# Turning the normed residual with VectorE blocks and a trip through DRAM instead of TensorE transposes

## The chip, the cores and the metric

The kernel runs on one core of one Trainium2 chip. Five engines work side by side, each through its own queue in order: TensorE (PE; its weight loads are listed as PEld), VectorE (DVE), ScalarE (ACT), GpSimd (POOL) and SyncE (SP). In this kernel nearly all DMAs are issued by SP, and an issue that waits for a semaphore holds up every issue behind it. The metric is the device time of the core in microseconds, the median of several executions.

## The reference

One transformer block in fp32 over 2048 tokens of 1024 features, with a single attention head of 256 features:

```python
x = x + layernorm(attn(layernorm(x)))
x = x + layernorm(ffn(layernorm(x)))

# attn: qkv = x @ Wqkv + bqkv; softmax(q k^T / 16) @ v; @ Wo + bo      (d = 256)
# ffn:  (silu(x @ W_gate.T) * (x @ W_up.T)) @ W_down.T                 (F = 2752)
# layernorm: (x - mean) / sqrt(var + 1e-5), no weights
```

The second layernorm's input is what this case is about. Its result, one row per token, has to be turned so that features lie on the partitions, because the gate and up matmuls sum over features.

## The kernel before

**Number format.** Each fp32 product is done as three fp32r matmuls (high times high, high times low, low times high). So operands are split into a high part (ScalarE copy, L110) and a low part (VectorE subtraction, L111) by `split`. The gate, up and down products are further cut by a Strassen scheme over halves of tokens, features and hidden units (`Pair`, `prod`, `sum_x`, `down_weights`).

**Tiles.** There are 16 tiles of 128 tokens (`NT`), in groups of four (`TB`), and 8 feature blocks of 128 (`NC_`).

**Attention stage (about 143 to 418 us).** The loop at L1201 runs over the 16 tiles in a software pipeline. Iteration i turns the softmax rows of tile i on TensorE (`turn`, L451; split by L110 and L111), computes the scores of tile i+1 (`scores`, L127 to L129, with a maximum on VectorE, L264), its softmax (`softmax`, L439 to L444, exponentials on ScalarE, L442), multiplies by v (`attend`, L467 and L468, into bank 6, read out by L469 and L470), turns the result (`turn_o`, L477, bank 5, read out by L479 and L480) and projects tile i-1 (`proj`, banks 5 and 7, read out by L490). For the first eight tiles (`EARLY`), iteration i also does the residual of tile i-2: `residual` normalizes the attention output in place (L504, ScalarE), adds x (L505, VectorE), stores the row as `x1_d` (L506, SP), takes its statistics (L117, L120 and L121 on VectorE; L122 and L508 on GpSimd) and writes the normed row over the attention output (L509, ScalarE). Then `xpose(i - 2)` turns that row.

**`xpose` before.** For each half of the features, four TensorE transposes (L599) go into one PSUM bank, a ScalarE copy (L601) brings it to the x tile, and one DMA (L603) stores it into `xT_d`, the turned matrix in DRAM. In the attention stage it borrows banks 6 and 5, in the gate-and-up stage banks 4 and 5, which are otherwise idle then.

**After the eight early tiles,** `first_load` (L613) and `first_sums` (L637, L661, L671) read `xT_d` of the first two groups back and build the Strassen operands in the last iterations of the attention loop.

**Gate-and-up stage of the first 1024 tokens (about 418 to 765 us).** The loop at L1312 runs over ten pairs of hidden blocks. Each pair issues 14 products of 12 matmuls (L866). Between products two background jobs run: `ahead(p)` turns the late tile of the pair before, loads the next late tile's attention output (`at_d`, L1294) and x (L1295) and forms weight sums (`down_weights`, L1010 and L880, stored by L1015); `behind(p)` loads weights (L1005) and does `residual` of the late tile (with L505 on GpSimd). So pairs 1 to 8 each do the residual of one of tiles 8 to 15, and the pair after each turns it. Weights stream through a ring of raw tiles (`raws`: `f4[4]`, `f2p`, `wr`; L769) into slots. Results are stored by `put` (L897).

**Order.** The tile framework's scheduler sets each engine's order from its own estimate of times, except where an instruction is pinned in program order (`pin`); the source order of the loops is therefore a guide and not the order of the queues.

**Buffers.** `pair[t % 3]` holds tile t's two rows: `a` (attention output, then normed row) and `xt` (x, then the residual). Late tiles use `f4[2]` and `f4[3]`.

Of the kernel before, what the change touches and what calls it, by code (L numbers as in the profile page):

```python
# [8 lines left out]
F32 = mybir.dt.float32  # L9
# [6 lines left out]
P = 128  # L16
T = 2048
C = 1024
D = 256
F = 2752  # L20
NT = T // P
# [3 lines left out]
TB = G // P  # L25
# [9 lines left out]
def block_kernel(ctx, tc, x, xt, wqk, wqk_t, wv, bqk, bv, wo, bo, wgu, wlast, wd, out):  # L35
# [12 lines left out]
    nc = tc.nc  # L48
# [4 lines left out]
    def tl(p, shape, dt, name):  # L53
        return p.tile(shape, dt, tag=name, name=name, bufs=1)
# [3 lines left out]
    ident = tl(cpool, [P, P], F32, "ident")  # L58
# [18 lines left out]
    bank = [tl(bank_pool, [P, 512], F32, f"bank{i}") for i in range(8)]  # L77

    dram = ctx.enter_context(tc.tile_pool(name="dram", bufs=1, space=bass.MemoryType.DRAM))
    q_d = [tl(dram, [P, 2, G], F32, f"q_d{g}") for g in range(NG)]  # L80
    mr_d = [tl(dram, [P, 2 * TB], F32, f"mr_d{g}") for g in range(NG)]
    xT_d = [tl(dram, [C, G], F32, f"xT_d{g}") for g in range(NG)]
    at_d = [tl(dram, [P, C], F32, f"at_d{t}") for t in range(NT)]
    x1_d = [tl(dram, [P, C], F32, f"x1_d{t}") for t in range(NT)]
    hd = [[{n: tl(dram, [P, 512], F32, f"hd{s}_{p}_{n}") for n in HS} for p in range(NPAIR)] for s in range(2)]
    xs_d = [[tl(dram, [P, C], F32, f"xs_d{c}_{k}") for k in range(2)] for c in range(NC_ // 2)]
    td = [{n: tl(dram, [P, 512], F32, f"td{p}_{n}") for n in ("T1", "T2", "T3", "T4")} for p in range(NPAIR)]
# [7 lines left out]
    f4 = [tl(cpool, [P, C], F32, f"f4_{i}") for i in range(5)]  # L95
# [17 lines left out]
    def norm_stats(halves, pin=None):  # L113

        s = small_tile()
        for i, h in enumerate(halves):
            b = nc.vector.bn_stats(s[:, 6 * i : 6 * i + 6], h)  # L117
            if pin:
                pin(b)
        nc.vector.bn_aggr(s[:, 12:14], s[:, 0:12])  # L120
        nc.vector.tensor_scalar(s[:, 14:15], s[:, 13:14], EPS, None, ALU.add)  # L121
        nc.gpsimd.tensor_tensor(s[:, 15:16], s[:, 14:15], mhalf, ALU.pow)  # L122
        return s[:, 12:13], s[:, 15:16], s
# [133 lines left out]
    def scores(i, j, pin=lambda i: i):  # L257

        cols = slice((i % TB) * P, (i % TB + 1) * P)
        q = qa if i < TB else qs[(i // TB) % 2]  # L260
        for d in range(2):
            k = kT(d, j)
            mm3(bank[j], (q[:, d, 0, cols], q[:, d, 1, cols]), (k[:, 0, :], k[:, 1, :]), d == 0, d == 1, pin)
        nc.vector.tensor_reduce(ys[i % 4][:, j : j + 1], bank[j], AX.X, ALU.max)  # L264
# [153 lines left out]
    pair = [(f4[0], f4[1]), (f4[2], f4[3]), (f2p[0], f2p[1])]  # L418
# [3 lines left out]
    EARLY = 2 * TB  # L422
# [5 lines left out]
    def q_load(g):  # L428
        nc.sync.dma_start(qraw, q_d[g])
# [6 lines left out]
    def softmax(i):  # L436

        s = ys[i % 4]
        nc.vector.tensor_reduce(s[:, 4:5], s[:, 0:4], AX.X, ALU.max)  # L439
        nc.vector.tensor_scalar(s[:, 5:6], s[:, 4:5], -1.0 / 16.0, None, ALU.mult)  # L440
        for j in range(4):
            nc.scalar.activation(p_s[:, j * 512 : j * 512 + 512], bank[j], AF.Exp, bias=s[:, 5:6], scale=1.0 / 16.0, accum_out=s[:, 8 + j : 9 + j])  # L442
        nc.vector.tensor_reduce(s[:, 12:13], s[:, 8:12], AX.X, ALU.add)
        nc.vector.reciprocal(s[:, 13:14], s[:, 12:13])  # L444

    def turn(i, j):

        b = bank[(4, 7)[j % 2]]
        for n in range(4):
            k = 4 * j + n  # L450
            nc.tensor.transpose(b[:, n * P : (n + 1) * P], p_s[:, k * P : (k + 1) * P], ident)  # L451
        d = pT[i % 2][:, 4 * j : 4 * j + 4, :, :]
        split(d[:, :, 0, :], d[:, :, 1, :], b.rearrange("p (n q) -> p n q", n=4))
# [41 lines left out]
    def out_stats(t, a):  # L495

        m, r, s = norm_stats([a[:, 0:512], a[:, 512:1024]], tc.keep_in_program_order if t >= EARLY else None)
        nc.gpsimd.tensor_scalar(s[:, 16:17], m, r, -1.0, ALU.mult, ALU.mult)
        return r, s

    def residual(t, a, xt, st=None, pin=lambda i: i):

        r, s = st or out_stats(t, a)
        pin(nc.scalar.activation(a, a, AF.Identity, bias=s[:, 16:17], scale=r))  # L504
        (nc.gpsimd if t >= EARLY else nc.vector).tensor_tensor(xt, xt, a, ALU.add)  # L505
        nc.sync.dma_start(x1_d[t], xt)  # L506
        m, r, s = norm_stats([xt[:, 0:512], xt[:, 512:1024]])
        nc.gpsimd.tensor_scalar(s[:, 16:17], m, r, -1.0, ALU.mult, ALU.mult)  # L508
        nc.scalar.activation(a, xt, AF.Identity, bias=s[:, 16:17], scale=r)  # L509
# [81 lines left out]
        pin(nc.vector.tensor_tensor(wo_s[:, d, 1, :], wr[d], f32(wo_s[:, d, 0, :]), ALU.subtract))  # L591


    def xpose(t, a, b, banks):
        for hf in range(2):
            o = banks[hf]
            for j in range(4):
                cb = 4 * hf + j
                nc.tensor.transpose(o[:, j * P : (j + 1) * P], a[:, cb * P : (cb + 1) * P], ident)  # L599
            s = b[:, hf * 512 : hf * 512 + 512]  # L600
            nc.scalar.copy(s, o)  # L601
            d = xT_d[t // TB][hf * 512 : hf * 512 + 512, (t % TB) * P : (t % TB + 1) * P]
            nc.sync.dma_start(d.rearrange("(j p) t -> p j t", p=P), s.rearrange("p (j t) -> p j t", j=4))  # L603

    def two(t):
        return t.rearrange("p (j n) -> p j n", j=2)
# [56 lines left out]
    def first_load(cb, r1, r2):  # L663
        load_xq(r1, 0, cb)
        load_xq(r2, 1, cb)
# [68 lines left out]
    class Slot:  # L734
        t = None
# [440 lines left out]
    X, Y = bank[0:4], bank[4:8]  # L1176
# [24 lines left out]
    for i in range(NT):  # L1201
        more = i + 1 < NT
        if i % TB == 0 and TB <= i < NT - TB:
            q_load(i // TB + 1)
        turn(i, 0)
        turn(i, 1)
        if i == NT - 1:
            for f in order[:2]:
                f.use()
            for f, r in zip(order[4:6], f4[2:4]):  # L1210
                f.load(r)
        if more:
            scores(i + 1, 0)
            scores(i + 1, 1)
        turn(i, 2)
        turn(i, 3)
        if more:
            scores(i + 1, 2)
            scores(i + 1, 3)
            softmax(i + 1)  # L1220

        if i < 2:
            wo_split(i)
        if i == 1:
            q_load(1)
        if i == 2:
            q_split(1, pin)
        if i % TB == 0 and TB <= i < NT - TB:
            q_split(i // TB + 1, pin)
        if 2 <= i < EARLY + 2:  # L1230
            residual(i - 2, *pair[(i - 2) % 3], sts[i - 2], pin)
        if i < EARLY:
            nc.sync.dma_start(pair[i % 3][1], x[i * P : (i + 1) * P, :])
        if i == NT - 1:
            for f in order[2:5]:
                f.use()
            for f, r in zip(order[6:8], (wr[1], f4[1])):
                f.load(r)
        if i > 0:
            turn_o(i - 1)  # L1240
        attend(i)
        if i > 0:
            proj(i - 1)
        if 2 <= i < EARLY + 2:
            xpose(i - 2, *pair[(i - 2) % 3], (bank[6], bank[5]))
        if 0 < i <= EARLY:
            sts[i - 1] = out_stats(i - 1, pair[(i - 1) % 3][0])
        cb = i - EARLY - 3
        if 0 <= cb < 4:
            first_sums(cb, *room[cb % 2])  # L1250
        if 0 <= cb + 1 < 4:
            first_load(cb + 1, *room[(cb + 1) % 2])
        if i == NT - 4:
            feed.pump()
        if i == NT - 2:
            for n in range(2):
                slots.free(flat(a2[:, 2 * n : 2 * n + 2, :, :]))
            feed.pump()
            order = [t2[0], t13[0], t13[1], t13[2], t2[1], t13[3]] + t4
            spare = f4[2], f4[3], wr[1], xe  # L1260
            for f, r in zip(order, spare):
                f.load(r)
# [17 lines left out]
    def late(p):  # L1280
        return EARLY + p - 1 if 1 <= p <= NT - EARLY else None

    def ahead(p):
        if p == 0:
            with tc.issue_after(last_o[0].ins):
                for n in range(5, 8):
                    order[n].use()
                    if n == 5:
                        order[9].load(f4[3])
            return  # L1290
        if late(p - 1):
            xpose(late(p - 1), *f4[2:4], Y[0:2])
        if late(p):
            nc.sync.dma_start(f4[2], at_d[late(p)])  # L1294
            nc.sync.dma_start(f4[3], x[late(p) * P : (late(p) + 1) * P, :])  # L1295
        down_weights(p - 1)

    def behind(p):
        if p == 0:
            for n in range(8, 10):  # L1300
                order[n].use()
            raws2.free(wr[1])
            raws2.free(bo_s)
        with tc.issue_after(pairs[1][0].loading.ins) if p == 0 else nullcontext():
            load_down(p)
        if late(p):
            residual(late(p), *f4[2:4])

    for s in range(2):
        pairs, rest, dn = half[s]  # L1310
# [70 lines left out]
```

## Time and profile before

| What | Value |
|---|---|
| Median of 3 runs | 1659.46 us (1659.44 to 1659.66) |
| Span of the profiled execution, first to last instruction | 1658.2 us |
| Rest of the time, outside that span (median less span) | 1.3 us |
| TensorE busy | 1647.1 us, 99% |
| VectorE busy | 1104.2 us, 67% |
| ScalarE busy | 734.7 us, 44% |
| GpSimd busy | 108.2 us, 7% |
| Mean granted TensorE clock | 0.999 |
| DMA traffic | 283.62 MB, mean 171 GB/s |

The profile is one execution; its own time is given by its span, and 1.3 us more lie around it. Busy shares are means over stages. A line such as L866 can be that of a helper through which many products go. In the chain of waits a row gives its start, its length and the engine and line. "Idle before" names what ended an engine's wait.

### The profile page before, as it was taken

The page shows a single profiled execution, that of the slowest core. Times are in us where ns is not written, and L with a number is a line of the kernel's source. Part 1 is how long each engine was busy: PE and PEld are TensorE (multiplying, and loading weights), DVE is VectorE, ACT ScalarE, POOL GpSimd, SP SyncE. Part 2 cuts the span into 40 slices and gives each one's busy share as a digit, 9 for nine tenths or more (in the row PEclk, how much of TensorE's full clock was granted, in tenths as well). Part 3 has the DMA queues.
Part 4 walks back from the last instruction along what each step waited for, and adds up shares of the span by engine and source line. Part 5 has one row for each costly group of instructions (what it writes and reads, how often), then busy time and mean ns, then how long its engine had stood idle before and what let it go on. Part 6 is the DMA issues. An engine that isn't in the chain of part 4 may idle for free.

```text
span 1658.2 us, 21110 instructions
## 1 busy us (share of the span) xinstructions
PE 1647.1 (99%) x7704; PEld 1374.3 (83%) x7704; DVE 1104.2 (67%) x1660; ACT 734.7 (44%) x1093; POOL 108.2 (7%) x157
## 2 busy tenths in 40 slices
PE   9999999999999999999999999999999999999998
PEld 8888888888888888888888888888888888888887
DVE  6756677768777777777587458955556665455458
ACT  5663555445544444444365344433333333354342
POOL 3120000000011111111000001100000000000001
PEclk9999999999999999999999999999999999999999
DMA  8451123435656666556477656533222233686653
GB/s 318 167 177 65 62 91 114 151 123 185 235 186 219 216 213 220 196 197 231 141 236 265 192 195 213 193 134 105 95 96 95 96 104 119 228 264 198 196 185 123
DMA packets 137689, 283.62 MB, mean 171 GB/s; under 512 B 14320, under 2 KB 31344, under 8 KB 137584
## 3 DMA queue, kind: packets, MB, share of 16 engines
q1 hardware_dynamic: 136432, 280.30, 50.6%
q10 hardware_dynamic: 1152, 1.97, 0.3%
q8 instruction: 60, 0.98, 0.2%
q14 instruction: 45, 0.37, 0.1%
HBM read 198.31 MB, written 83.90 MB: 170 GB/s over the span
## 4 chain that ended last, share of the span: by engine, by line
PE 96%; DMA 1%; DVE 1%; issue 1%; ACT 0%; SPq 0%; POOL 0%; POOLq 0%; DVEq 0%
PE bank L866 72%; PE bank L127 4%; PE bank L129 4%; PE bank L128 4%; PE bank L467 3%; PE bank L468 2%; PE bank L451 2%; PE bank L245 1%; PE bank L246 1%; PE bank L599 1%; PE bank L310 1%; DMA f<-wv 0%; PE bank L1052 0%; PE bank L1051 0%; PE bank L463 0%
## 5 line engine op out<-in xcount | busy, mean ns | idle before, releaser
L866 PE MATMUL bank<-a 128*128 128x512 f32 (+1 forms) x960 | 226.4, 386 | 0.0
L866 PE MATMUL bank<-xb,a 128*128 128x512 f32 x912 | 212.5, 389 | 0.5 <-DVE a L111 0.5
L866 PEld LDWEIGHTS bank<-a 128*128 128x128 f32 x960 | 179.0, 188 | 36.6
L866 PEld LDWEIGHTS bank<-xb,a 128*128 128x128 f32 x912 | 170.9, 188 | 36.2 <-DVE a L111 0.9
L110 ACT CAST a<-f2p 128x1024 fp32r<-128x1024 f32 (+2 forms) x123 | 107.0, 870 | 113.0 <-PE bank L866 86.3
L111 DVE TENSOR_TENSOR a<-f2p,a 128x1024 fp32r<-128x1024 f32 (+2 forms) x123 | 122.3, 994 | 45.2 <-ACT a L110 40.9
L111 DVE TENSOR_TENSOR a<-f,a 128x1024 fp32r<-128x1024 f32 (+1 forms) x70 | 78.5, 1122 | 103.5 <-ACT a L110 101.3
L866 PE MATMUL bank<-kx,a 128*128 128x512 f32 x612 | 146.0, 389 | 0.0
L866 PEld LDWEIGHTS bank<-kx,a 128*128 128x128 f32 x612 | 114.9, 188 | 23.9
L866 PE MATMUL bank<-wvo 128*128 128x512 f32 (+1 forms) x498 | 120.9, 386 | 0.0
L880 DVE TENSOR_TENSOR p_s<-bank,p_s 128x512 f32<-128x512 f32 x96 | 65.0, 681 | 77.1 <-PE bank L866 47.7
L866 PEld LDWEIGHTS bank<-wvo 128*128 128x128 f32 x498 | 92.9, 188 | 18.9
L110 ACT CAST a<-f 128x1024 fp32r<-128x1024 f32 (+1 forms) x70 | 57.8, 825 | 103.3 <-PE bank L866 101.8
L866 PE MATMUL bank<-kx,wvo 128*128 128x512 f32 x420 | 100.1, 389 | 0.0
L866 PE MATMUL bank<-a,a 128*128 128x512 f32 x420 | 99.4, 389 | 0.0
L866 PEld LDWEIGHTS bank<-kx,wvo 128*128 128x128 f32 x420 | 78.8, 188 | 16.4
L866 PEld LDWEIGHTS bank<-a,a 128*128 128x128 f32 x420 | 78.8, 188 | 16.4
L111 DVE TENSOR_TENSOR wvo<-f,wvo 128x1024 fp32r<-128x1024 f32 (+1 forms) x47 | 54.6, 1162 | 51.0 <-ACT wvo L110 51.0
L866 PE MATMUL bank<-a1b,wvo 128*128 128x512 f32 x360 | 86.6, 389 | 0.0
L866 PEld LDWEIGHTS bank<-a1b,wvo 128*128 128x128 f32 x360 | 67.6, 188 | 14.0
L866 PE MATMUL bank<-kx 128*128 128x512 f32 (+1 forms) x339 | 78.5, 387 | 0.0
L866 PEld LDWEIGHTS bank<-kx 128*128 128x128 f32 x339 | 63.4, 188 | 13.0
(330 smaller groups left out, 3075.5 us busy)
## 6 DMA issues: line engine op xcount, KB each, us to landing
f2p<-wgu SPq DMA_DIRECT2D x41, 512.0 KB, 5.5
hd_S<-p_s SPq DMA_DIRECT2D x60, 256.0 KB, 4.7
f<-x SPq DMA_DIRECT2D x28, 512.0 KB, 4.2
f<-wgu SPq DMA_DIRECT2D x22, 512.0 KB, 3.5
wr<-wgu SPq DMA_DIRECT2D x21, 512.0 KB, 5.8
f<-wd SPq DMA_DIRECT2D x20, 512.0 KB, 5.1
hd_A<-xi SPq DMA_DIRECT2D x40, 256.0 KB, 2.0
td_T<-f SPq DMA_DIRECT2D x40, 256.0 KB, 4.5
```

The source lines that it names most:

```text
L110: nc.scalar.copy(hi, src)
L111: (lo_engine or nc.vector).tensor_tensor(lo, src, f32(hi), ALU.subtract)
L127: pin(nc.tensor.matmul(o, w[0], m[0], start=first, stop=False))
L128: pin(nc.tensor.matmul(o, w[0], m[1], start=False, stop=False))
L129: return pin(nc.tensor.matmul(o, w[1], m[0], start=False, stop=last))
L245: pin(nc.tensor.matmul(b, xg[:, c, 0, cols], wv_s[:, c, :, :].rearrange("p a f -> p (a f)"), start=(c == 0), stop=False))
L246: pin(nc.tensor.matmul(b[:, D:], xg[:, c, 1, cols], wv_s[:, c, 0, :], start=False, stop=(c == 7)))
L451: nc.tensor.transpose(b[:, n * P : (n + 1) * P], p_s[:, k * P : (k + 1) * P], ident)
L467: nc.tensor.matmul(b, p[:, k, 0, :], vt(k).rearrange("p h d -> p (h d)"), start=(k == 0), stop=False)
L468: nc.tensor.matmul(b[:, D:], p[:, k, 1, :], vt(k, 0), start=False, stop=(k == NKB - 1))
L866: one = nc.tensor.matmul(o, w[i], m[j], start=first and n == 0, stop=last and n == 2, skip_group_check=chained)
L880: nc.vector.tensor_tensor(o, a, b, op)
```

## The change

The eight TensorE transposes of a tile, their PSUM banks and the two ScalarE copies are gone. VectorE can turn 32x32 blocks within groups of 32 partitions, which is not a full transpose, so the rows are regrouped first. `regroup` writes the normed row to a new DRAM tensor `xn_d[t]` with its four quarters of 256 features on four groups of rows (512 pieces of 1 KB) and reads it back over the residual row: partition `32 i + s` then holds feature quarter i of the four tokens `4 s` to `4 s + 3`. `xpose` is one VectorE StreamTranspose of 128x1024 that writes with a step of four elements, and one DMA stores the result into `xT_d`. The features come out in the order block j, quarter i, column c, so the rows of the gate and up weights are permuted on the host in the same way (`rows`); layernorm has no weights that would need it.

In the attention loop `regroup` of tile i-2 follows its residual, `xpose` moves one iteration later (tile i-3), and the x row of tile i is loaded after that, since it takes the buffer. In the gate-and-up stage `regroup` follows the residual in `behind`, and `xpose` stays in the `ahead` of the next pair. The scheduler then orders the queues anew: in the attention iterations of the early tiles the orders of TensorE, VectorE, ScalarE and SP all differ; in the gate-and-up stage VectorE gains one instruction a pair in front of L1010, and on SP the read-back stands after the stores of S1 to S4 and before one weight load, while the load of `at_d` moves behind the store of `xT_d`.

```diff
+    xn_d = [tl(dram, [P, C], F32, f"xn_d{t}") for t in range(NT)]
...
-    def xpose(t, a, b, banks):
-        for hf in range(2):
-            o = banks[hf]
-            for j in range(4):
-                cb = 4 * hf + j
-                nc.tensor.transpose(o[:, j * P : (j + 1) * P], a[:, cb * P : (cb + 1) * P], ident)
-            s = b[:, hf * 512 : hf * 512 + 512]
-            nc.scalar.copy(s, o)
-            d = xT_d[t // TB][hf * 512 : hf * 512 + 512, (t % TB) * P : (t % TB + 1) * P]
-            nc.sync.dma_start(d.rearrange("(j p) t -> p j t", p=P), s.rearrange("p (j t) -> p j t", j=4))
+    def regroup(t, a, b):
+
+        nc.sync.dma_start(xn_d[t].rearrange("(i s) (g c) -> i s g c", i=4, g=4).rearrange("i s g c -> (s g) i c"), a.rearrange("p (i c) -> p i c", i=4))
+        nc.sync.dma_start(b, xn_d[t])
+
+    def xpose(t, a, b):
+
+        nc.vector.transpose(a.rearrange("p (j s g) -> p g j s", j=8, g=4), b.rearrange("p (g j c) -> p g j c", g=4, j=8))
+        d = xT_d[t // TB][:, (t % TB) * P : (t % TB + 1) * P]
+        nc.sync.dma_start(d.rearrange("(j p) t -> p j t", p=P), a.rearrange("p (j t) -> p j t", j=8))
...
             residual(i - 2, *pair[(i - 2) % 3], sts[i - 2], pin)
-        if i < EARLY:
-            nc.sync.dma_start(pair[i % 3][1], x[i * P : (i + 1) * P, :])
+            regroup(i - 2, *pair[(i - 2) % 3])
+        if i < 3:
+            nc.sync.dma_start(pair[i][1], x[i * P : (i + 1) * P, :])
...
-        if 2 <= i < EARLY + 2:
-            xpose(i - 2, *pair[(i - 2) % 3], (bank[6], bank[5]))
+        if 3 <= i < EARLY + 3:
+            xpose(i - 3, *pair[i % 3])
+        if 3 <= i < EARLY:
+            nc.sync.dma_start(pair[i % 3][1], x[i * P : (i + 1) * P, :])
...
         if late(p - 1):
-            xpose(late(p - 1), *f4[2:4], Y[0:2])
+            xpose(late(p - 1), *f4[2:4])
...
             residual(late(p), *f4[2:4])
+            regroup(late(p), *f4[2:4])
...
-    wgt, wut = np.asarray(L0_ffn_W_gate).T, np.asarray(L0_ffn_W_up).T
+    rows = np.arange(C).reshape(4, 8, 32).transpose(1, 0, 2).reshape(C)
+    wgt, wut = np.asarray(L0_ffn_W_gate).T[rows], np.asarray(L0_ffn_W_up).T[rows]
```

## The prediction

> **What bounds the kernel now.** I read the page's busy shares and chain first, then the chain of waits within two stages, then the timelines of VectorE and ScalarE around one residual, then the DMA issues.
>
> ```profile
> span 1658.2 us, 21110 instructions
> ...
> PE 1647.1 (99%) x7704; PEld 1374.3 (83%) x7704; DVE 1104.2 (67%) x1660; ACT 734.7 (44%) x1093; POOL 108.2 (7%) x157
> ...
> PE 96%; DMA 1%; DVE 1%; issue 1%; ACT 0%; SPq 0%; POOL 0%; POOLq 0%; DVEq 0%
> ```
>
> TensorE is busy for 99% of the span and carries 96% of the chain. Work taken off TensorE shortens the kernel, unless another engine then arrives late. The chain in the gate-and-up stage of the first half of the tokens:
>
> ```profile
> 491.76 0.87 PE bank L599 x8
> 492.64 38.10 PE bank L866 x168
> 530.74 0.87 PE bank L599 x8
> ```
>
> The eight transposes of a tile stand between matmuls without a gap: one pair of this stage lasts 38.97 us (530.74 - 491.76), of which 168 matmuls take 38.10. The chain in the attention stage:
>
> ```profile
> 232.32 0.44 ACT a L110
> 232.81 0.60 ACT f2p L601
> 233.45 0.50 PE bank L467
> ```
>
> Here TensorE also waits for ScalarE's copy (L601), because `attend` needs bank 6 back. The windows from 198 to 317 us show TensorE busy 118.13 of 119.00 us, so these waits are 0.87 us in all.
>
> **What it removes.** Sixteen tiles, eight transposes each.
> - Gate and up, 8 tiles: 8 x 0.88 (38.97 less 38.10, rounded) = 7.1 us.
> - Attention, 8 tiles: 8 x 0.87 = 6.96, and the 0.87 us of waits: 7.8 us. Blocks of L599 start 17.0 us apart (197.9 to 317 us, seven steps); without them TensorE needs 17.0 - 0.87 - 0.12 = 16.0 us a tile.
> - ScalarE loses 32 copies of 0.59 us (18.9 us), SP half of its 32 transposed stores; neither is on the path.
>
> Gross gain: 14.9 us.
>
> **What it adds.** Per tile: one StreamTranspose of 128x1024 on VectorE, a 512 KB write of the normed rows and a 512 KB read back (`regroup`), the read waiting on SP for the write, the transpose waiting on VectorE for the read. The permuted weight rows cost nothing on the chip: same shapes and transfers.
>
> *Duration of the transpose.* No row shows one. Below: VectorE's 128x1024 operations, 1.22 us (L505). Above: a copy over 128x1024 whose elements lie 32 bytes apart, against an ordinary one:
>
> ```profile
> L204 ACT ACTIVATE f<-f 128x1024 f32<-128x1024 f32 x10 | 10.5, 1050 | 0.0
> L220 ACT COPY f2p<-f2p 128x1024 f32<-128x1024 f32 x3 | 6.6, 2184 | 0.2 <-DMA f2p<-mr_d 0.2
> ```
>
> The stride doubles it (2.18 against 1.05). `xpose` writes each element 16 bytes from the last, so I take 2.2 us, nearest to L220, and keep 1.2 to 2.5 (1.22 times L220's ratio of 2.08). [...]
>
> *Gate and up: hidden.* In the changed program the transpose stands before the four weight sums that begin with L1010. After those VectorE is idle:
>
> ```profile
> 533.69 1.42 DVE L880 TENSOR_TENSOR f<-f,f 128x512 f32<-128x512 f32 x2
> 540.68 1.23 DVE L111 TENSOR_TENSOR a<-f,a 128x1024 fp32r<-128x1024 f32 x1 [5.58 <-ACT a L110]
> ```
>
> The normed rows are done at 524.5 (L509: 523.23 + 1.24). Write and read at 4.5 to 5.1 us each (rows of 512 KB in this stage) land at 533.5 to 535; VectorE is at the spot at 532.3. Wait 1.2 to 2.7, transpose 2.2: 3.4 to 4.9 us, under the 5.58. Were this cover gone, the delay would enter the dense 25 us behind it, where bank `cg` is read at 548.0 and needed by TensorE at 553.4: 5 us more before TensorE notices. On SP the read-back stands before one weight load (`wr0`, issued 527.3, used about 20 us later) and two stores; the load of `at_d` moves behind the xT store (issue about 541 instead of 531.6, landing 4.5 later, used by L117 at 545.0), a lateness of about 1 us within the same cover. SP's wait for L509 also comes ahead of the store of S1, so L902's copy, which waits for a store now (3.1 us), may wait 2 to 3 us longer; its bank is needed 6 us later. I cost all this at 0, and 0 to 5 us for the range.
>
> *Attention: not hidden.* VectorE is busy 84.45 of 119 us here, 12.1 of 17.0 per tile; with 2.2 it is 14.3 of 16.0. It keeps up in sum; the order is the trouble. One residual and its row statistics:
>
> ```profile
> 238.27 1.23 DVE L505 TENSOR_TENSOR f<-f,f 128x1024 f32<-128x1024 f32 x1 [0.78 <-ACT f L504]
> 239.45 0.69 DVE L111 TENSOR_TENSOR a<-bank,a 128x512 fp32r<-128x512 f32 x1
> 240.05 1.28 DVE L117 BATCH_NORM_STATS2 small<-f 128x6 f32<-128x512 f32 x2
> ```
>
> ```profile
> 243.98 1.24 ACT L509 ACTIVATE f<-f,small 128x1024 f32<-128x1024 f32 x1 [1.54 <-POOL small L508]
> ```
>
> From the start of L505 to the end of L509 is 6.95 us here; the eight tiles give 6.5 to 7.9, mean 7.0. The transfers of this stage:
>
> ```profile
> x_d<-f SPq DMA_DIRECT2D x6, 512.0 KB, 3.3
> f<-x SPq DMA_DIRECT2D x4, 512.0 KB, 3.6
> ```
>
> In the changed program the transpose of tile t stands *before* L505 of tile t+1 on VectorE, which is in order. So a loop closes: L505(t), norm, write, read, transpose(t), what stands between, L505(t+1). It takes 7.0 + 3.3 + 3.6 + 2.2 = 16.1 us and what lies between, counted from the order at 0.60 us a 512-column and 1.14 us a 1024-column operation (starts of successive rows): 1.5, 3.2, 0, 0.1, 0.9 and 2.0 us for the six steps from tile 0 to tile 6. Behind the waiting transpose are queued the low parts of the softmax rows (L111), L264, L505 and L470, and L470 is what TensorE's next `turn_o` waits for, some 0.5 us after it would be ready. Against TensorE's 16.0 the six steps are late by 0.1 x 6 + 7.7 = 8.3 us. Part is absorbed: L505 starts are 14.2 to 19.8 us apart today without TensorE waiting, so the phase has play; I take 2 us once (0 to 4). Tiles 6 and 7 have no such step: tile 6's transpose comes a whole tile later, tile 7's stands before no residual. Their waits (`at_d` store before tile 6's, loads of `xT_d` before L637) are of the kind that VectorE takes today with up to 2.2 us idle at L637 and no wait on TensorE. Cost: 8.3 - 2 = 6.3 us.
>
> **Sum.** -7.1 - 7.8 + 6.3 = -8.6 us. The profiled execution spans 1658.2 us; the runs' median of 1659.46 lies 1.3 us above, outside the first and last instruction and untouched. 1659.5 - 8.6 gives 1651. A change under 0.2% (3.3 us) counts as none.
>
> **Rivals.**
> - *The transpose runs at full speed* (1.2 us). For: it reads contiguously, and VectorE's rows of that length take 1.22. Against: the strided row. The steps become 15.1 + between; only the 3.2 and 2.0 steps exceed 16.0 clearly, about 4 us less the play: 2. Time: 1659.5 - 14.9 + 2 = 1646.5. Chance 0.24.
> - *The DMA round trip decides, and the kernel gets slower.* For: the chain near 1016 us holds a store of 4.45 us followed by a load of 4.23, 8.9 us up to VectorE's start, with DMA busier. Against: in the attention stage DMA is busy 34% and loads take 3.5 to 4.0. Each extra us costs six. At 8.9 instead of 6.9 the attention stage is late by 8.3 + 12 - 2 = 18.3: +3.4, 1663. From that point on it is slower. Other ways in: L509 standing behind two or three exponentials on ScalarE for tiles 2, 3 and 5 (0.7 us each). Chance 0.15.
> - *Only the gate-and-up gain remains, partly*: round trip 7.7 and 2.2 us, attention late by 11, or the gate-and-up cover fails by some us. 1659.5 - 14.9 + 11 = 1655.6, up to 1660. Chance 0.17.
> - That the transposes stay is excluded: the changed order has no L599 or L601.
>
> **Numbers.** My forecast has 0.44. Range 1645 (full speed, nothing lost) to 1663 (round trip 8.9). Faster by over 0.2%: forecast and first rival, 0.68; within: 0.17; slower: 0.15.
>
> **What would show it.** Right: pairs of the gate-and-up stage 38.1 us apart; StreamTranspose near 2.2 us; in the attention stage VectorE idle before it, released by the read of `xn_d`, and TensorE waiting 4 to 8 us in all for L470 or the low parts. Wrong: TensorE without waits there (1646), transposes of 4 us, a store-to-load trip near 9 us, or TensorE waiting in the gate-and-up pairs.

## The result, and the profile after

The changed kernel takes 1671.6 us (median of 4 runs, 1670.1 to 1671.9) against 1659.45 us in the same comparison: ratio 1.0072, 95% interval 1.0058 to 1.0086. It is 12 us slower where 8.6 us less was forecast. In what follows the line numbers are those of the changed kernel, one higher than before from L110 on (L505 is now L506, L866 is L867, L902 is L903, L117 is L118). First the page:

```profile
span 1669.7 us, 20815 instructions
...
PE 1640.0 (98%) x7576; PEld 1361.9 (82%) x7576; DVE 1133.6 (68%) x1676; ACT 718.5 (43%) x1061; POOL 110.5 (7%) x157
...
PE 73%; DVE 11%; DMA 9%; issue 3%; ACT 1%; POOL 1%; SPq 1%; DVEq 0%; POOLq 0%; ACTq 0%
```

The 128 transposes are gone from TensorE, but its share of the chain fell from 96% to 73%. VectorE and DMA now carry a fifth of the chain, as they would if TensorE waited for a loop through several engines. The waits of TensorE (line waited, releaser: us in total, times, longest):

```profile
PE bank L867 <- ACT p_s L903: 11.5, 6, 3.0
PE bank L478 <- DVE ys L440: 3.0, 3, 1.6
PE bank L478 <- DVE f L471: 1.7, 2, 1.4
```

The last two belong to the attention stage, where 4 to 8 us of waits were forecast. The first was priced at nothing, and all of it lies in the gate-and-up stage.

**Where the time went.** The last read-out of the attention stage, before and after, in VectorE's timeline (start, length, then the instruction):

```profile
419.62 0.74 DVE L490 SCALAR_TENSOR_TENSOR xe<-bank,ys,bo_s 128x512 f32<-128x512 f32 x1
```

```profile
418.22 0.75 DVE L491 SCALAR_TENSOR_TENSOR xe<-bank,ys,bo_s 128x512 f32<-128x512 f32 x1
```

So the attention stage is 1.4 us ahead. From there to the end of the gate-and-up stage the same instructions fall from 1.4 us ahead to 10.7 us behind, and the rest of the kernel adds 0.8: 11.5 us in the spans. So nearly the whole miss is in the gate-and-up stage. The eight late transposes start 41.15 us apart on average (495.06 to 783.11, seven steps), against 38.1 that TensorE needs.

**One pair of that stage.** VectorE's timeline (in brackets the idle time before, and what ended it):

```profile
574.13 0.69 DVE L881 TENSOR_TENSOR p_s<-bank,p_s 128x512 f32<-128x512 f32 x1 [4.10 <-ACT p_s L903]
...
577.24 2.00 DVE L602 STREAM_TRANSPOSE f<-f 128x1024 f32<-128x1024 f32 x1 [1.62 <-DMA f<-xn_d]
...
585.05 1.22 DVE L112 TENSOR_TENSOR a<-f2p,a 128x1024 fp32r<-128x1024 f32 x1
588.33 1.29 DVE L118 BATCH_NORM_STATS2 small<-f 128x6 f32<-128x512 f32 x2 [2.07 <-DMA f<-at_d]
```

and SP's queue of the same pair (start, time in the queue):

```profile
571.31 0.40 SPq L898 DMA_DIRECT2D hd_S<-p_s  x1
571.80 0.41 SPq L598 DMA_DIRECT2D f<-xn_d  x1
...
579.27 0.37 SPq L604 DMA_DIRECT2D xT_d<-f  x1
579.73 0.53 SPq L1299 DMA_DIRECT2D f<-x  x1
580.36 2.18 SPq L1016 DMA_DIRECT2D td_T<-f  x3
582.77 0.85 SPq L1298 DMA_DIRECT2D f<-at_d  x1
```

Follow it round. The read of `xn_d` goes out at 571.80, behind the last store of S (571.31). It lands, and the transpose runs at 577.24. Its store goes out at 579.27, and the load of `at_d` at 582.77, since it overwrites the row that this store still reads (such a store lands after 3.5 us in the median). VectorE waits 2.07 us for that load before L118 at 588.33. Behind L118 stand some 20 us of dense VectorE work, whose last results are the S stores of the next pair; the next read goes out at 611.56. Before, no wait of VectorE in this stage was on a load; `at_d` was issued long before it was needed (SP, then VectorE):

```profile
531.64 0.32 SPq L1294 DMA_DIRECT2D f<-at_d  x1
545.01 1.28 DVE L117 BATCH_NORM_STATS2 small<-f 128x6 f32<-128x512 f32 x2
```

TensorE meets the new loop mainly at one place (11.5 of its 13.2 us of waits in this stage): ScalarE's copy L903 waits for a store of S, and a later product needs the bank that it reads.

### The profile page after: what moved, and what is told of

It reads as the page before. It is cut to its first block, busy times and chain, and to the rows that moved or that the text cites. A ratio compares the mean times of both kernels' runs of the same rounds, so it can differ in the third digit from the quotient of the medians.

```text
span 1669.7 us, 20815 instructions
## 1 busy us (share of the span) xinstructions
PE 1640.0 (98%) x7576; PEld 1361.9 (82%) x7576; DVE 1133.6 (68%) x1676; ACT 718.5 (43%) x1061; POOL 110.5 (7%) x157
## 4 chain that ended last, share of the span: by engine, by line
PE 73%; DVE 11%; DMA 9%; issue 3%; ACT 1%; POOL 1%; SPq 1%; DVEq 0%; POOLq 0%; ACTq 0%
PE bank L867 56%; PE bank L128 3%; PE bank L130 3%; PE bank L129 3%; DVE a L112 2%; DMA f<-xn_d 2%; PE bank L468 2%; DMA td_T<-f 2%; DVE p_s L881 2%; PE bank L246 1%; DVE small L118 1%; DVE wvo L112 1%; PE bank L452 1%; PE bank L469 1%; DVE f L602 1%
## 5 line engine op out<-in xcount | busy, mean ns | idle before, releaser
L867 PE MATMUL bank<-a 128*128 128x512 f32 (+1 forms) x960 | 226.4, 386 | 0.0
L867 PE MATMUL bank<-xb,a 128*128 128x512 f32 x912 | 212.4, 389 | 1.3 <-DVE a L112 1.3
L867 PEld LDWEIGHTS bank<-a 128*128 128x128 f32 x960 | 179.0, 188 | 36.6
L867 PEld LDWEIGHTS bank<-xb,a 128*128 128x128 f32 x912 | 170.9, 188 | 37.0 <-DVE a L112 1.7
L111 ACT CAST a<-f2p 128x1024 fp32r<-128x1024 f32 (+2 forms) x123 | 107.0, 870 | 127.9 <-PE bank L867 87.8
L867 PE MATMUL bank<-kx,a 128*128 128x512 f32 x612 | 147.7, 390 | 0.0
L867 PEld LDWEIGHTS bank<-kx,a 128*128 128x128 f32 x612 | 115.3, 188 | 24.1
L867 PE MATMUL bank<-wvo 128*128 128x512 f32 (+1 forms) x498 | 120.9, 386 | 0.0
L867 PEld LDWEIGHTS bank<-wvo 128*128 128x128 f32 x498 | 92.9, 188 | 18.9
L867 PE MATMUL bank<-kx,wvo 128*128 128x512 f32 x420 | 100.1, 389 | 0.0
L867 PE MATMUL bank<-a,a 128*128 128x512 f32 x420 | 99.6, 389 | 0.3 <-ACT xi L928 0.3
L111 ACT CAST a<-f 128x1024 fp32r<-128x1024 f32 (+1 forms) x70 | 57.5, 822 | 90.2 <-PE bank L867 88.8
L867 PEld LDWEIGHTS bank<-a,a 128*128 128x128 f32 x420 | 78.7, 188 | 17.1 <-ACT xi L928 0.7
L867 PEld LDWEIGHTS bank<-kx,wvo 128*128 128x128 f32 x420 | 78.8, 188 | 16.4
L867 PE MATMUL bank<-a1b,wvo 128*128 128x512 f32 x360 | 87.2, 390 | 1.5 <-DVE xi L881 1.4
L867 PEld LDWEIGHTS bank<-a1b,wvo 128*128 128x128 f32 x360 | 67.3, 188 | 16.8 <-DVE xi L881 2.8
L867 PE MATMUL bank<-kx 128*128 128x512 f32 (+1 forms) x339 | 78.5, 387 | 0.0
L867 PEld LDWEIGHTS bank<-kx 128*128 128x128 f32 x339 | 63.4, 188 | 13.0
```

What stands on the lines that cost most here:

```text
L111: nc.scalar.copy(hi, src)
L867: one = nc.tensor.matmul(o, w[i], m[j], start=first and n == 0, stop=last and n == 2, skip_group_check=chained)
```

## The experiments

Two theories were set against each other. *Theory 1:* the loop just described sets the pair, and the late `at_d` load is the part of it that is too much. *Theory 2:* the write of `xn_d`, which SP now issues in front of the S stores, delays them and with them L903. "Apart" below is the mean distance of the eight late transposes in the run's own trace.

| Run | Edit | Apart, us | Median, us | Ratio to before (interval) |
|---|---|---|---|---|
| changed kernel | | 41.15 | 1671.6 | 1.0072 (1.0058 to 1.0086) |
| e1 | `at_d` load earlier | 38.77 | 1652.5 | 0.996 (0.9946 to 0.9974) |
| e2 | write issued by ScalarE | 42.27 | 1680.7 | 1.0124 (1.0109 to 1.0139) |
| e3 | late tiles by TensorE | | 1658.0 | 0.9987 (0.9977 to 0.9996) |
| e4 | late transpose twice | 42.94 | 1685.4, one run | |
| e7 | e1, late transpose twice | 40.82 | 1670.7, one run | |
| e6 | contiguous write | 40.55 | 1664.2, one run | |
| e5 | e1, early transposes later | 38.30 | 1652.1 | 0.9944 (0.9931 to 0.9956) |
| e9 | e5, weight sums first | 38.14 | 1648.4 | 0.9926 (0.9912 to 0.9939) |
| e10 | e9, tile 6 in a row of its own | 38.11 | 1648.4 | 0.9927 (0.9915 to 0.994) |
| e11 | e10, contiguous, rows permuted at stores | 38.09 | 1686.6 | 1.0162 (1.0148 to 1.0176) |
| e12 | e11, plain output store | 38.16 | 1646.8 | 0.9926 (0.9913 to 0.9938) |
| e13 | e10, contiguous, four reads | 38.83 | 1651.2 | 0.9952 (0.994 to 0.9964) |

The medians of the kernel before beside these runs were 1660.1 to 1660.6 us.

**e1: the load of at_d first.**

```diff
-            xpose(late(p - 1), *f4[2:4])
+            xpose(late(p - 1), f4[3], f4[2])
-            regroup(late(p), *f4[2:4])
+            regroup(late(p), *f4[2:4], into=f4[2])
```

> Edit: in the gate-and-up stage the read-back goes into the row that was written (f4[2]) and the transpose into f4[3], so that the load of at_d waits for the transpose and no longer for the landing of the xT store; on SP only the at_d load and the x load change places, no other engine's order changes. Theory 1 (a loop of period 40.5 us through VectorE: read of xn_d, transpose, load of at_d, L118, 20 us of dense work, last store of S, next read): the at_d load goes out near 3.0 us earlier (538.7 instead of 541.7), the 2 to 3.2 us of VectorE's idle time before L118 go, the loop becomes 37.5 us, under TensorE's 38.1, so pairs are 38.1 us apart, L867 does not wait for L903, and the median is 1650 to 1655 us. Theory 2 (the write of xn_d in front of the S stores on SP holds ScalarE's copy L903, and the idle time at L118 is slack): pairs stay near 40.5 us, 1668 to 1672 us.

Measured: 1652.5 us, 19 us less than the changed kernel, by a swap of two rows, through which two loads change places on SP. What VectorE waited for in the gate-and-up stage, in the changed kernel and then in e1:

```profile
DVE p_s L881 <- ACT p_s L903: 28.7, 8, 4.7
DVE small L118 <- DMA f<-at_d: 18.0, 7, 3.4
```

```profile
DVE p_s L881 <- ACT p_s L903: 29.8, 9, 4.5
DVE f L602 <- DMA f<-xn_d: 22.6, 8, 4.1
```

The 18.0 us for `at_d` are gone. L903 keeps VectorE waiting as long as ever, yet TensorE's waits for it fell from 11.5 us to

```profile
PE bank L867 <- ACT p_s L903: 1.3, 2, 1.0
```

So the store is only where TensorE meets the loop. The write still stands in front of the S stores, so theory 2 falls here. One number was off: pairs are 38.77 us apart, not 38.1. VectorE still falls behind by 0.7 us a pair, 4.7 us over the seven steps, and TensorE hardly notices within ten pairs.

**e2: the write from ScalarE's queue.** `regroup` of the late tiles issues its write with `nc.scalar.dma_start`.

> Edit: in the gate-and-up stage ScalarE's queue issues the write of xn_d right behind L510, so it no longer stands in front of the S stores on SP; the orders of TensorE, VectorE and GpSimd are unchanged. Theory 1 (loop through VectorE by way of the at_d load): the S stores go out at most 0.7 us earlier, and with them the read of xn_d; pairs 39.8 to 40.5 us, 1666 to 1672 us. Theory 2 (the write in front of the S stores is what holds L903): the stores go out 1 to 1.5 us earlier or more, L903 no longer comes late, pairs near 38.1 us, 1650 to 1657 us.

Measured: 1680.7 us, outside both expectations. The S stores did go out right behind their data, but the write itself took more than twice as long, by the DMA issues of this stage (KB each, median us to landing), first in the changed kernel, then in e2:

```profile
xn_d<-f SPq DMA_DIRECT2D x7, 512.0 KB, 3.7
```

```profile
xn_d<-f ACTq DMA_DIRECT2D x7, 512.0 KB, 8.2
```

Its landing is what the read waits for, and the pair lengthened by 1.1 us. Whether the queue or the S stores in flight beside it made the write slow was not separated. As a test of theory 2 the run is not clean, since the S stores out of `p_s` landed later as well (5.5 us in the median instead of 4.9), and TensorE's waits for L903 came to 13.2 us. It fits theory 1: a longer trip adds to the pair.

**e3: late tiles by TensorE again.** Early tiles keep the new way.

> Edit: tiles 8 to 15 are turned by TensorE, ScalarE and two stores as in the kernel before (L510 writes their columns in the new feature order), tiles 0 to 7 by the new way. Theories 1 and 2 alike: the attention stage keeps its gain of 1.4 us, and the gate-and-up stage takes what it took before: 1658.0 us, 1657 to 1659. Theory 3 (the loss comes from the attention stage's new order, which hands over the gate-and-up stage out of phase): still above 1665 us.

Measured: 1658.0 us, and in its trace the attention stage ends 1.3 us ahead and the gate-and-up stage gives back 0.4 of it. The attention stage hands nothing bad on: theory 3 falls.

**e4 and e7: the transpose twice,** in the changed kernel and in e1.

```diff
+            nc.vector.transpose(<same target>, <same source>)
             xpose(late(p - 1), ...)
```

> Edit: in the gate-and-up stage the transpose is done twice in a row, same source and target; nothing else moves. Theory 1 (loop through VectorE): each pair after the first two becomes longer by the added 1.9 us, 42.4 us apart; 7 to 8 pairs: +13 to +16, 1684 to 1688 us. Theory 2 (stores hold L903, VectorE has cover): 1671 to 1675 us.

> Edit: e1 with the transpose of the gate-and-up stage done twice. Theory 1 (a loop; in e1 it takes 37.5 us by the sum, against TensorE's 38.1): it becomes 39.4 us, pairs lengthen by 1.3 us, 8 pairs: +10, 1660 to 1665 us; if e1 has no spare time at all, +1.9 a pair and 1668. Theory 2 (VectorE has cover): 1652 to 1654 us.

Measured: 1685.4 and 1670.7 us. The distance grows by 1.79 us in the first (42.94 less 41.15) and by 2.05 in the second (40.82 less 38.77): in both kernels all or nearly all of the added instruction lies in the loop, and VectorE's idle time shields little of it. e7 came out above its main expectation and near the branch "no spare time at all": the 37.5 us that I had worked out for e1's loop was 1.3 too short.

**e6: the write without a step.** The target becomes `a.rearrange("p (g j s) -> p g j s", ...)`; tokens within a tile come out in another order.

> Edit, on top of the changed kernel: all 16 transposes write their elements one behind the other and not with a step of four; so the tokens within a tile end up in another order, everything else is kept. If the step is what makes the transpose slow (2.03 us against 1.22 us for an ordinary VectorE operation on 128x1024): 1.1 to 1.3 us, and by theory 1 the pairs shorten by 0.8 us to 39.7, attention by 1 to 3 us: 1661 to 1666 us. If the transpose itself takes two cycles an element: 2.0 us, and 1671 to 1673 us.

Measured: 1664.2 us. The transposes of the changed kernel and of e6 (ns: minimum, median, maximum):

```profile
L602 DVE STREAM_TRANSPOSE f<-f x14: 1994/2025/2069, 203.1 to 783.1; 128x1024 f32<-128x1024 f32 x14
```

```profile
L602 DVE STREAM_TRANSPOSE f<-f x14: 1245/1245/1248, 203.2 to 775.3; 128x1024 f32<-128x1024 f32 x14
```

Without the step it costs about what the residual addition of the same size costs (L506, 1.22 us). The 16-byte step adds 0.78 us (2.025 less 1.245). Without it pairs shorten by 0.6 us, and the attention stage ends 3.6 us earlier than in the changed kernel, a little more than expected.

**e5 and e9: the attention loop, and more room.** e5 puts the transpose of an early tile one iteration later, behind the low part of `turn_o` and the softmax maximum. e9 also puts the late transpose behind the four weight sums. Both leave one thing out: tile 6's row is overwritten by the projected row of tile 8 before it is turned, so they are read for the order of work alone.

```diff
-        if 3 <= i < EARLY + 3:
-            xpose(i - 3, *pair[i % 3])
+        if 4 <= i < EARLY + 3:
+            with tc.issue_after(last_o[1].ins), tc.issue_after(last_max[0].ins):
+                xpose(i - 4, *pair[(i - 1) % 3][::-1])
...
+            with tc.issue_after(down_weights(p - 1).ins):
+                xpose(late(p - 1), f4[3], f4[2])
```

> Edit, on top of e1: in the attention stage too the read-back goes into the row that was written, the transpose of tile t writes the other row, and it stands one iteration later on VectorE, right behind the low part of the turned attention output (turn_o) and behind the softmax maximum, where VectorE waits 1.3 to 1.9 us for TensorE, and no longer in front of the residual addition of tile t+1. Theory A (the loop residual, norm, write, read, transpose, next residual costs TensorE the 5 to 6 us of waits for L471 and L440 between 198 and 420 us): these waits go, the stage ends 5 to 8 us earlier than in the kernel before instead of 1.4 to 1.9, and the median is 1646 to 1649 us. Theory B (the 2.0 us of added VectorE work are what holds TensorE, wherever they stand): the waits stay 5 to 6 us, 1651 to 1654 us.

> Edit, on top of e5_late_transpose: in the gate-and-up stage the transpose stands behind the four weight sums, not in front of them, so the 3 to 4 us that VectorE waits for the read of xn_d hold 2.8 us of work. Theory 1 (a loop through VectorE that has no spare time left in e1): the last waits of L867 (1.3 us in all) go, and the loop gains 2.8 us of spare time: 0.5 to 2 us less than e5_late_transpose. Theory 2 (no loop left in e1, the waits come from the stores): the same time as e5_late_transpose within 0.5 us.

Measured: 1652.1 and 1648.4 us. In e5's trace the attention stage ends 4.6 us ahead (1.9 in e1), a little under what theory A expected, and TensorE's idle time between 198 and 420 us fell from 5.6 us in e1 to 3.6. So the loop of theory A is there, but it accounts for some 2 to 3 of the 5 to 6 us. The median alone would not show it: it lies in the range of theory B, and 0.4 us under e1. Its five times spread from 1648.1 to 1652.8 us; the profiled one was the shortest, and TensorE is busy in it for all of 350 us of the gate-and-up stage. e9's lie within 1647.9 to 1649.1. The weight sums fill the wait for the read, which drops from 22.7 us over 9 waits in the whole kernel to 2.9 over 5, so the stage hangs less on the landing of one transfer. By the medians this was worth 3.6 us, more than the 0.5 to 2 that theory 1 expected. The two profiled executions do not show where, since that of e5 is the shorter one: what e5's longer executions waited for is not recorded.

**e10: both loops opened, all tiles turned.**

> Edit: e9_sums_first, with tile 6's row read back into its other row and turned out of it, since the row that e9_sums_first uses for tile 6 is overwritten by the projected row of tile 8 before it is turned. The orders of TensorE and ScalarE are those of e9_sums_first. Theories A and 1 together (both loops opened): the time of e9_sums_first, 1647 to 1650 us; by theory B or 2 nothing else is expected.

Measured: 1648.4 us, 12 us under the kernel before. VectorE in the attention stage, the changed kernel first, then e10 (where L604 is the transpose, L508 the residual addition):

```profile
240.63 2.03 DVE L602 STREAM_TRANSPOSE f2p<-f2p 128x1024 f32<-128x1024 f32 x1 [0.70 <-DMA f2p<-xn_d]
242.51 1.21 DVE L506 TENSOR_TENSOR f<-f,f 128x1024 f32<-128x1024 f32 x1
```

```profile
231.21 2.06 DVE L604 STREAM_TRANSPOSE f<-f 128x1024 f32<-128x1024 f32 x1
240.60 1.23 DVE L508 TENSOR_TENSOR f<-f,f 128x1024 f32<-128x1024 f32 x1 [0.78 <-ACT f L507]
```

In the first the residual stands behind the transpose of the tile before and its read. In the second the transpose does not wait for its read, the residual stands 9 us behind it, and its 0.78 us are a wait for ScalarE, as in the kernel before. The page of e10:

```profile
span 1646.7 us, 20822 instructions
...
PE 94%; DMA 2%; DVE 2%; issue 1%; ACT 1%; SPq 0%; POOL 0%; POOLq 0%; DVEq 0%; ACTq 0%
```

**e11, e12, e13: the contiguous write as well.**

> Edit, on top of e10_both_loops: the transpose writes its elements one behind the other (1.245 us in e6_contiguous_write instead of 2.03); the tokens of a tile then stand in the order g, s instead of s, g, which the store of x1_d and the output store make good by permuting whole rows. If both loops are open, TensorE's remaining waits in the attention stage (1.8 for L471's line and 1.2 us for a low part) shrink with VectorE's 0.78 us less per tile, and nothing else is left to gain: 0.5 to 2.5 us less than e10_both_loops. If one loop still binds (8 tiles at 0.78 us in it): 4 to 6 us less.

> Edit: e11_contiguous without the permutation in the output store, so the output's rows stand in another order within a tile; all else as there. If the permuted output store is what made e11_contiguous slow (its attention and gate-and-up stages were not: TensorE busy 118.5 of 119, 102.2 of 103, 350 of 350 us): 1644 to 1647 us, that is e10_both_loops less the 2.8 us of TensorE's waits that e11_contiguous saved between 198 and 420 us. If the permuted store of x1_d or the new token order did it: 1680 us or more still.

> Edit, on top of e10_both_loops: the transpose writes its elements one behind the other, and the tokens come out in their own order because the trip groups other tokens (32 g + s, not 4 s + g): the rows are written to xn_d as they are and read back by four transfers of 128 KB, each to 32 partitions; the stores of x1_d and of the output are as in the kernel before. If four small reads land as soon as one large (SP needs 1.2 us more to issue them): 1645 to 1648 us. If they land later by more than the 2.8 us that the order of e9_sums_first left to spare in the gate-and-up loop, pairs get longer than 38.1 us and the time goes above 1650.

Measured: 1686.6, 1646.8 and 1651.2 us. e12 points the way that e6 promised: 1.5 us below e10 by the medians, less than the 2.8 expected and not clear of its spread (1645.9 to 1651.7). Its output rows stand in another order within a tile, and paying for the token order takes the gain back. In e11 the permuted output stores take longer in the queue already, by the DMA instructions of the output line on ScalarE's queue (ns), e11 then e12:

```profile
L1108 ACTq DMA_DIRECT2D out<-x x8: 547/1424/3195, 1638.9 to 1665.4; - x8
```

```profile
L1108 ACTq DMA_DIRECT2D out<-x x8: 338/338/380, 1620.2 to 1640.8; - x8
```

After the last of them e11 runs on for 19 us, e12 for 3. Another 18 us of e11's loss fall between 880 and 1230 us, where SP stores the first half's rows. The two kernels differ in these stores alone, so they are the cause; how they hold TensorE up was not followed. In e13 the four small reads land after 6.7 us, against 6.4 for one in e10, but three more issues stand in front of the last, and VectorE waits for the reads again (18.5 us over 7, against 1.4 over 3 in e10), as it does for `at_d` (7.4 us over 7). Pairs are 38.83 us apart: the second branch of the expectation.

## Why the prediction was wrong

- **What TensorE no longer does: right.** 128 transposes are gone from the stages named. In e10, where no lateness comes in between, the gate-and-up stage is 7.1 us shorter by the starts of the same matmuls, as forecast (8 x 0.88 is 7.0; the sum had 7.1).
- **Duration of the transpose: right.** 2.03 us, 2.2 taken. That 0.78 us of it come from the write step is shown by e6 (1.245 us without it).
- **Attention, not hidden: right in mechanism and size.** Forecast -7.8 + 6.3 = -1.5 us, measured -1.4. The residual additions L506 of tiles 0 and 6 start 104.5 us apart (189.76 and 294.25), where the loop gave 6 x 16.1 + 7.7 = 104.3; single steps are off by up to 1.0 us, and the differences cancel. TensorE waits about 6 us there, in the 4 to 8 expected, for L471, the low parts and above all (3.0 us) the softmax maximum, which was not named as a releaser. e10 opened this loop and got some 3 us back.
- **Gate and up, "hidden, cost 0": the step that failed.** Forecast -7.1 us, measured +12.1. The wait for the read and the 2.0 us of the transpose were sized about right for one pair. Two things were wrong. First, the load of `at_d` was put "within the same cover". In the kernel before, the cover of 5.58 us lies in front of L111 at 540.68, and L117, which needs the load, stands 4.3 us behind it. The issue at 541 was right (541.70 in one pair), but the landing took 5.8 us in the median instead of 4.5, and the wait at L118 comes on top: 18.0 us over seven pairs. e1 took away this one cause and 19 us went. Second, I counted the chain once and against the schedule of the kernel before. It closes over the pair: what L118 loses, the S stores and the next read lose too. So "5 us more before TensorE notices" was no reserve per pair but one for the whole stage. At 3.05 us a pair (41.15 less 38.1) it lasts under two pairs. TensorE noticed first at another bank that the prediction named, that of ScalarE's copy (L902 before, L903 now), "needed 6 us later". In the kernel before, the copy ends at 529.86 and TensorE's next product in its bank starts at 534.18: 4.3 us, and 0.87 less without the eight transposes in between. In the changed kernel the first wait for it comes in the pair of the second late transpose; the copy before, then copy and product in the changed kernel:

```profile
529.27 0.59 ACT L902 COPY p_s<-bank 128x512 f32<-128x512 f32 x1 [3.13 <-DMA hd_S<-p_s]
```

```profile
532.96 0.59 ACT L903 COPY p_s<-bank 128x512 f32<-128x512 f32 x1 [5.23 <-DMA hd_S<-p_s]
533.60 1.66 PE L867 MATMUL bank<-qa,a 128*128 128x512 f32 x6 [2.23 <-ACT p_s L903]
```

- **Not in the sum: the clock.** See below; about 3.0 us of the 12.
- **The range** reached 1663 by way of a slow round trip in the attention stage. "TensorE waiting in the gate-and-up pairs" stood among the signs of a wrong forecast but had a price of some us, because no rival closed the loop there.

Not settled: the gate-and-up stage lost 19.2 us (12.1 plus the 7.1 that it should have gained). By the starts of successive matmuls in the trace, nine gaps in front of L867 make 14.6 of them and the slower clock 3.0; the other 1.6 us are spread over gaps too short to be told from the ordinary step.

## What to carry to other kernels

When a change adds a step to work that recurs, close the loop: add up everything from the step round to itself through the orders of the queues, the landings of its transfers included, and compare that with what the bound engine needs (here 41.15 against 38.1 us). Idle time seen on an engine covers a delay only if it stands in front of the instruction that is delayed (here 5.58 us stood in front of L111, and the 18.0 us of waits came at L118 behind it), and play between engines is spent once, not once a round (here 4.3 us less 0.87, used up at 3.05 us a pair). A buffer that a new step keeps a little longer can move a load that nobody counted; here swapping source and target of the transpose was worth 19 us.

## What the runs showed of the hardware that was not expected

**The clock after a wait.** TensorE's timeline in the changed kernel: six matmuls of one kind, then six after the longest wait, then the next six.

```profile
649.85 1.52 PE L867 MATMUL bank<-qa,a 128*128 128x512 f32 x6
...
655.96 2.93 PE L867 MATMUL bank<-qa,a 128*128 128x512 f32 x6 [3.01 <-ACT p_s L903]
658.68 2.76 PE L867 MATMUL bank<-qb,a 128*128 128x512 f32 x6
```

After 3.01 us of waiting the same work takes almost twice as long. The granted clock is 0.5 for 6.8 us (655.15 to 661.98): it falls while TensorE still waits, and the 6.0 us of it that TensorE works in cost 3.0 us more. So this wait came to about twice its length. After the two waits of 2.2 us in the same trace the clock stayed at 1.00. The mean granted clock of the profiled execution is 0.995 in e4 (longest wait of TensorE 2.9 us), 0.997 in the changed kernel (3.0) and in e2 (2.3), 0.998 in e6 (3.0), and 0.999 in e7 (2.2) and in the kernel before (1.4). What decides which wait lowers the clock was not shown.
